# More buffers for adj's blocks and signs, a fifth group of kept products, and new costs in the planner of a two-layer graph kernel

## The chip, the cores and the metric

The kernel runs on one core of a Trainium2 chip. The metric is the device time of one execution in microseconds (us), the median of three runs. A core has a matrix engine (TensorE: PE for its matmuls, PEld for its weight loads in the profile), three engines for elementwise work (VectorE = DVE, ScalarE = ACT, GpSimd = POOL), a queue that issues transfers (SyncE = SP), and 16 DMA engines that carry the transfers of all queues.

## What is computed

Inputs are `x` (2708 nodes, 256 features, float32) and a sparse matrix `adj` (2708 by 2708) whose entries are zero or lie in 0.05 to 1, with a full diagonal. There are two layers. Cut to what matters:

```
# layer 0
A  = adj without its diagonal,  d = diagonal
n1 = GRU_edge(A @ x,  x)                          # gates from support @ Wih.T and x @ Whh.T
for each of 3 heads:  hW = x @ W;  hp = (A > 0) @ hW
    e = leaky_relu([hp, 0] @ a);  att = softmax(where(A > 0, e, very negative))
    s += (att * A) @ hW
n2 = GRU_node(s / 3, x)
x  = layernorm(x + d * n1 + d * n2)
# layer 1
h  = x @ W (4 heads of 64);  e = leaky_relu(src_i + dst_j) where adj_ij > 0.5
x  = layernorm(x + softmax_over_i(e).T @ h + bias)
```

A GRU cell needs six products for each of its 256 features: support times `Wih` and x times `Whh`, for each of three gates (r, z, n). The x products don't depend on the graph, so they can be made at any time once `x` and `Whh` are on the chip.

## The kernel before, in words

The 2708 nodes make 22 blocks of 128 (`NB`), and the blocks make six groups of up to 512 columns (`CH`; the last is 148 wide). The work has three stages, though they overlap.

**Stage 1, the sweep over adj.** For each group `g` and each pair of row blocks, 11 pairs to a group, a block of 2 x 128 x 512 of the transposed adj (512 KB) is loaded into `at2`. ScalarE makes two bf16 signs of it: `over2` (entry over a half) and `mask2` (entry nonzero). In between, GpSimd clears the diagonal in the blocks that have it. VectorE takes a maximum for each 64 columns (`found0`). TensorE multiplies `only` by `over2` into the bank `dbs[0]` and `u3` by `mask2` into `accs[0]`. After a group, `logits`, `flags` and `listed` turn the sums into lists of the rows that are nonzero in each 64-column tile (`idx0`), so that later stages gather these rows alone. Buffers: `at` has 4, `over` 2 and `mask` 2, all in the 24 KB-a-partition region `home1`.

Beside the sweep, `keep` makes x's GRU products of the first `KEPT` = 4 groups: for each of 2 cells, 2 halves of the features and 3 gates, two float32 matmuls of 128x512 into `accs[1]` or `dbs[1]`, in turn; a copy to one of three `kept` buffers (ScalarE for two of three, VectorE for the third); and a 256 KB store to `XH` in HBM. The weights `Whh` are loaded early; the weights `Wih` (`w_i`, 768 KB for each of the two cells) sit in the list `loads`, which the sweep empties one entry a pair, although they are first used by stage 2.

**Stage 2, layer 0.** For each 64-column tile, rows of x (with the attention weights) are gathered from HBM by index (POOL `rows`), scaled by the entries (`prepared`), and multiplied into `accs` (`multiplied`), the denominators into `dbs`; `divided` ends a tile. The first tile takes `accs[0]` and `dbs[0]`, the second `accs[1]` and `dbs[1]`, and so on in turn, so the second tile can't start before the last `keep` has left its banks. When the tiles of a group are done, `cells_and_norm` multiplies by the head weights (`supports`: 12 matmuls), runs both GRU cells, normalises, and writes the table for layer 1. A group below `KEPT` reads its x products back from `XH` and adds them on VectorE; a group from `KEPT` on makes them on TensorE.

**Stage 3, layer 1.** The same for 128-column tiles: gather, four weightings on VectorE for each tile of rows (`weighed`), four matmuls (`attended`), normalise, store.

**The order.** No engine's order is written out by hand. Every operation is first recorded by a `Plan`, with what it reads and writes (`note`), and a duration and a latency from `Plan.cost`. `Plan.issue` then plays a simulated clock: at each step it takes the engine that is free first and, among its ready operations, the one with the longest remaining chain, with a bonus for TensorE to stay with the operand type that it has (`STAY`) and a charge for changing it (`SWITCH`). That fixes the order of the instructions on each engine; on the chip an engine works through its list and waits when an operand isn't there. The constants matter for the change: `LOAD` (latency of a transfer), the latency of an indirect gather, and TensorE's costs by type and size. Since all instructions are emitted from the one call in the recorder, the profile gives every one of them the line L217 (or L1842 for the frame); they are told apart by tile names and shapes. `home1` to `home4` all appear as `f_home`.

Of the kernel before, what the change touches and what calls it, by code (L numbers as in the profile page):

```python
# [10 lines left out]
F32 = mybir.dt.float32  # L11
BF16 = mybir.dt.bfloat16
# [8 lines left out]
P = 128  # L21
D = 256
KD = D // P
HEADS0 = 3
HEADS1 = 4
C1 = D // HEADS1
# [4 lines left out]
CH = 512  # L31
# [67 lines left out]
class Plan:  # L99
# [7 lines left out]
    JOINED = 16  # L107
    ENGINES = ("tensor", "vector", "scalar", "gpsimd", "sync")
    LAG = 0.08
    LOAD, RATE, QUEUED = 2.2, 250.0e3, 4.0  # L110
    SWITCH, STAY = {"scalar": 1.3, "tensor": 0.2}, {"tensor": 5.0}
    TABLES = {AF.Sigmoid: 1, AF.Tanh: 1, AF.Exp: 2, AF.Sqrt: 3}

    def __init__(self, nc):
# [36 lines left out]
    def cost(self, engine, method, out, ins, kwargs):  # L151

        n = max(self.count(v) for v in [out] + ins)
        if method == "indirect_dma_start":
            return 1.25, 3.0
        if method == "dma_start":
            size = 4
            for _, k in tuple(out.ap):
                size *= k
            return 0.08 if engine == "sync" else 0.25, self.LOAD + size / self.RATE  # L160
        if engine == "tensor":
            n = self.count(out)
            if ins[0].dtype == BF16:
                t = max(0.06, n / 2000)
            else:
                t = max(0.22 if ins[0].ap[-1][1] <= C1 + 1 else 0.43, n / 590)
            return t, t + 0.1
        by_partition = any(isinstance(kwargs.get(k), bass.AP) for k in ("bias", "scale"))
        if engine == "scalar":
            t = 0.09 + n / 1200 + 0.1 * by_partition  # L170
        elif engine == "gpsimd":
            t = 0.1 + n / (1300 if method == "memset" else 320)
        elif method == "reciprocal":
            t = 0.07 + n / 160
        else:
            pairs = all(v.dtype == BF16 and tuple(v.ap)[-1] == (1, 2) for v in [out] + ins)
            t = 0.06 + n / (1900 if pairs else 3800 if method == "memset" else 960)
            t += 0.065 * (method == "scalar_tensor_tensor")
        return t, t + 0.08
# [127 lines left out]
def fast_path(ctx: ExitStack, tc: tile.TileContext, i: dict, out: bass.AP, bad: bass.AP):  # L307
# [11 lines left out]
    nc = plan = Plan(tc.nc)  # L319
# [27 lines left out]
    const = ctx.enter_context(tc.tile_pool(name="f_const", bufs=1))  # L347
# [3 lines left out]
    def ring(tiles):  # L351

        return cycle(tiles).__next__
# [14 lines left out]

    TS = dram.tile([NG, HEADS1, CH], F32, name="f_TS")

    KEPT = 4
    XH = dram.tile([KEPT * 2 * KD * 3 * P, CH], F32, name="f_XH")
    plan.pitch = {XH.tensor.name: CH, T0.tensor.name: TW, T1.tensor.name: TW, TS.tensor.name: HEADS1 * CH}

# [73 lines left out]
    for t, of in ((less_room, TILES0 + TILES1), (less_whole, WHOLE0 + WHOLE1)):  # L448
        c = 0
        while c < len(of):  # L450
# [4 lines left out]
            c = e  # L455
# [237 lines left out]
    ap, tiles = Rings(const, 1, home2), Rings(const, 8, home1)  # L693
# [47 lines left out]
    def later_kd(src, wide, name):  # L741
        t = const.tile([P, KD, wide], F32, name=name)
        later(t, src.rearrange("(k p) n -> p k n", p=P))
        return t

    cells = []
    of_cells = ("edge", "node")
    w_hs = [later_kd(i[f"L0_gnn_{cell}_WhhT"], 3 * D, f"f_{cell}_wh") for cell in of_cells]
    later(xn[:, :GR, :], x[: GR * P, :].rearrange("(b p) d -> p b d", p=P))
    for cell, w_h in zip(of_cells, w_hs):  # L750
        w_i = later_kd(i[f"L0_gnn_{cell}_WihT"], 3 * D, f"f_{cell}_wi")
        b_i = const.tile([P, 3 * KD], F32, name=f"f_{cell}_bi")
        b_h = const.tile([P, 3 * KD], F32, name=f"f_{cell}_bh")
        later(b_i, i[f"L0_gnn_{cell}_bihT"])
        later(b_h, i[f"L0_gnn_{cell}_bhhT"])
        b_s = const.tile([P, 3 * KD], F32, name=f"f_{cell}_bs")
        cells.append((w_i, w_h, b_i, b_h, b_s))
# [48 lines left out]
    def head_weights(b0, b1):  # L806
        e = e_col[:, b0:b1, :]
        v = small.tile([P, NB * HEADS0], F32, name="e_v")[:, : (b1 - b0) * HEADS0]
        v = v.rearrange("p (b h) -> p b h", h=HEADS0)
        nc.vector.scalar_tensor_tensor(e, e, SLOPE, e, op0=ALU.mult, op1=ALU.max)  # L810
        nc.vector.tensor_scalar(v, e, SHIFT0 + REACH0, SHIFT0 - REACH0, op0=ALU.min, op1=ALU.max)
        nc.scalar.activation(Ew[:, b0:b1, :HEADS0], v, AF.Exp, bias=shift)
        split3(
            small, [E3[:, b0:b1, s * HEADS0 : (s + 1) * HEADS0] for s in range(3)],
            Ew[:, b0:b1, :HEADS0], P, (b1 - b0) * HEADS0, f"E_rest{b1 - b0}",
        )
        full = min(b1, NF)
        if full > b0:
            nc.sync.dma_start(
                T0[b0 * P : full * P, D:].rearrange("(b p) e -> p b e", p=P), Ew[:, b0:full, :]  # L820
            )
        if b1 > NF:
            nc.sync.dma_start(T0[NF * P :, D:], Ew[: size[last], NF, :])
# [28 lines left out]
    def keep(g, n, o, gate):  # L852
# [10 lines left out]
    keeps = [  # L863
        (g, n, o, gate) for g in range(KEPT) for n in range(2) for o in range(KD) for gate in range(3)
    ]

    for g, cs in enumerate(groups):
        w = width[g]
        pe, pf = accs[0], dbs[0]
        c0, nf = base[g] // W0, w // W0  # L870
        for b0 in range(0, NB, 2):
            pair = [b0, b0 + 1]
            at2 = tiles.tile([P, 2, CH], F32, name="at", bufs=4)
            over2 = tiles.tile([P, 2, CH], BF16, name="over", bufs=2)
            mask2 = tiles.tile([P, 2, CH], BF16, name="mask", bufs=2)
            for b in pair:
                if g == 0 and b % GR == 0:
                    load_xT(b // GR)
                    projected_u(b // GR)
            if loads and (g > 0 or b0 in (10, 16)):  # L880
                loads.pop(0)()
            for _ in range(1 if g < 2 else 2):
                if g > 0 and keeps:
                    keep(*keeps.pop(0))
            whole = size[b0 + 1] == P
            if whole:
                rows_of = adjT[b0 * P : (b0 + 2) * P, base[g] : base[g] + w].rearrange("(s p) n -> p s n", p=P)
                nc.sync.dma_start(at2[:, :, :w], rows_of)
            else:
                for b in pair:  # L890
                    nc.sync.dma_start(
                        at2[: size[b], b - b0, :w], adjT[b * P : b * P + size[b], base[g] : base[g] + w]
                    )
            parts = [(P, slice(0, 2))] if whole else [(size[b], slice(b - b0, b - b0 + 1)) for b in pair]
            for p, s in parts:
                nc.scalar.activation(over2[:p, s, :w], at2[:p, s, :w], AF.Sign, bias=minus_half[:p])
            for b in pair:
                if b in cs:
                    p, o = size[b], b * P - base[g]
                    v = at2[:p, b - b0, o : o + p]  # L900
                    nc.gpsimd.tensor_mul(v, v, off_diag[:p, :p])
            for p, s in parts:
                nc.scalar.activation(mask2[:p, s, :w], at2[:p, s, :w], AF.Sign)
                b1, b2 = b0 + s.start, b0 + s.stop
                nc.vector.tensor_reduce(
                    found0[:p, c0 : c0 + nf, b1:b2].rearrange("p c b -> p b c"),
                    at2[:p, s, : nf * W0].rearrange("p b (c i) -> p b c i", i=W0), AX.X, ALU.max,
                    apply_absolute_value=True,
                )
                if nf * W0 < w:  # L910
                    nc.vector.tensor_reduce(
                        found0[:p, c0 + nf : c0 + nf + 1, b1:b2].rearrange("p c b -> p b c"),
                        at2[:p, s, nf * W0 : w].rearrange("p b (c i) -> p b c i", c=1), AX.X, ALU.max,
                        apply_absolute_value=True,
                    )
            for b in pair:
                p = size[b]
                nc.tensor.matmul(
                    pf[:NB, :w], lhsT=only[:p, b, :], rhs=over2[:p, b - b0, :w], start=(b == 0), stop=(b == last)
                )  # L920
            for b in pair:
                p = size[b]
                nc.tensor.matmul(
                    pe[:H3, :w], lhsT=u3[:p, b, :], rhs=mask2[:p, b - b0, :w], start=(b == 0), stop=(b == last)
                )
        logits(g, pe)
        flags(g, pf)
        if g == NG - 3:
            while loads:
                loads.pop(0)()  # L930
            weights()
        if g == NG - 2:
            head_weights(0, groups[-1][0])
        listed(0, *ranked[0][g])
    head_weights(groups[-1][0], NB)
    plan.urgent = 0.0
    for batch, made in ranked[1]:
        listed(1, batch, made)
# [24 lines left out]
    rows, ready = {}, {}  # L963
# [888 lines left out]
```

## Time and profile before

| what | value |
|---|---|
| time, median of 3 | 910.15 us (910.13 to 920.45) |
| span of the profiled execution | 912.4 us, mean granted TensorE clock 0.945 |
| PE busy | 792.7 us, 3911 instructions |
| PEld busy | 494.4 us |
| DVE busy | 613.6 us |
| ACT busy | 548.7 us |
| POOL busy | 526.6 us |
| DMA | 132.41 MB, mean 145 GB/s |

"Busy" is the time in which an engine has an instruction in it, and for TensorE neighbouring matmuls overlap, so its share overstates how full it is. A float32 matmul stands in the trace as two instructions, a bf16 matmul as one. The DMA share is the mean over the 16 DMA engines.

The stages can be placed by their landmarks: the last load of adj is issued at 209.6 us, the last store of a kept product at 250.0 us, the first matmul with the head weights starts at 325.3 us, and GpSimd's first gather for layer 1 after a long wait starts at 744.0 us.

### The profile page before, as it was taken

What the parts mean: (1) busy time and instruction counts of PE and PEld (TensorE: products, weight loads), DVE (VectorE), ACT (ScalarE), POOL (GpSimd) and SP (SyncE); (2) the same over time, 40 slices, a digit from 0 to 9 for tenths busy, and PEclk for the clock granted to TensorE, in tenths of its full rate; (3) what the DMA queues carried; (4) which work ended last, traced back from release to release, by engine and by line L of the source; (5) the groups of instructions that cost most, each with busy time, mean ns of one, the idle gap of its engine ahead of it and who ended that gap; (6) DMA issues with size and microseconds to landing.
All of it is one profiled execution on the core that took longest, in us unless ns stands there. A gap on an engine that the chain in (4) does not pass through costs nothing. (4 is left out here: it accounts for less than half of the span.)

```text
span 912.4 us, 14024 instructions
## 1 busy us (share of the span) xinstructions
PE 792.7 (87%) x3911; PEld 494.4 (54%) x3911; DVE 613.6 (67%) x2051; ACT 548.7 (60%) x1552; POOL 526.6 (58%) x613
## 2 busy tenths in 40 slices
PE   4987889798989899988988997999899879988783
PEld 3532333344566645665446544645644468877782
DVE  6676679785366558785486547639713658999993
ACT  3779788765477854675357734745742333166687
POOL 3047867776777777677777776761410023577640
PEclk9899999999999999797998998999999999999995
DMA  8888889776533434543374435322310024665541
GB/s 323 274 273 252 243 236 312 226 201 172 154 104 105 134 74 128 161 109 92 85 218 140 119 83 166 91 64 87 83 53 0 4 60 122 180 179 179 148 125 45
DMA packets 85047, 132.41 MB, mean 145 GB/s; under 512 B 21520, under 2 KB 43880, under 8 KB 84320
## 3 DMA queue, kind: packets, MB, share of 16 engines
q1 hardware_dynamic: 63712, 84.26, 29.2%
q0 software_dynamic: 20320, 45.59, 19.8%
q10 hardware_dynamic: 928, 1.57, 0.5%
q8 instruction: 33, 0.54, 0.2%
q14 instruction: 54, 0.44, 0.2%
HBM read 113.03 MB, written 21.12 MB: 147 GB/s over the span
## 5 line engine op out<-in xcount | busy, mean ns | idle before, releaser
L217 POOL DMA_INDIRECT rows<-f_T,f_idx x254 | 254.9, 1003 | 222.4 <-PE side L217 87.0
L217 PE MATMUL acc<-four,rows 128*128 128x256 f32 (+1 forms) x712 | 193.6, 412 | 10.1 <-DVE f_home L217 5.5
L217 ACT ACTIVATE four<-four,rows 128x64 f32<-128x64 f32 (+1 forms) x534 | 145.9, 337 | 44.4 <-DMA rows<-f_T,f_idx 19.5
L217 PEld LDWEIGHTS acc<-four,rows 128*128 128x128 f32 x712 | 136.4, 203 | 48.4 <-issue 12.8
L217 POOL DMA_INDIRECT raw<-in_adj_dram,f_idx x91 | 89.4, 982 | 27.6 <-issue 18.0
L217 DVE TENSOR_REDUCE f_found<-f_home 128x16 f32<-128x1024 f32 (+4 forms) x84 | 72.1, 883 | 11.3 <-POOL f_home L217 7.4
L217 POOL DMA_INDIRECT f_xn<-in_adjT_dram,f_idx x63 | 66.4, 1055 | 22.5 <-issue 17.4
L217 POOL DMA_INDIRECT f_home<-in_adjT_dram,f_idx x67 | 64.8, 967 | 24.1 <-issue 14.0
L217 ACT ACTIVATE f_home<-f_home,f_minus_half 128x1024 bf16<-128x1024 f32 (+3 forms) x72 | 69.5, 976 | 10.6 <-DMA f_home<-in_adjT_dram 5.0
L217 PE MATMUL acc<-f_home,rows 128*65 128x128 f32 (+2 forms) x512 | 66.4, 283 | 10.3 <-DVE f_home L217 7.3
L217 ACT ACTIVATE f_home<-f_home 128x1024 bf16<-128x1024 f32 (+3 forms) x72 | 62.6, 880 | 15.3 <-PE acc L217 9.6
L217 PEld LDWEIGHTS acc<-f_home,rows 128*65 128x65 f32 (+1 forms) x512 | 56.0, 141 | 17.3 <-DVE f_home L217 10.3
L217 PE MATMUL side<-f_home,f_node_wi 128*128 128x512 f32 (+1 forms) x144 | 61.2, 560 | 1.1 <-DVE f_home L217 1.0
L217 DVE SCALAR_TENSOR_TENSOR f_home<-pl,rows,f_m 128x128 f32<-128x128 f32 x196 | 55.1, 338 | 5.9 <-DMA rows<-f_T,f_idx 5.6
L217 PE MATMUL side<-f_home,f_gat_w 128*128 128x512 f32 (+1 forms) x144 | 55.9, 544 | 1.9 <-DVE f_home L217 1.9
L217 PE MATMUL side<-f_home,f_edge_wi 128*128 128x512 f32 (+1 forms) x144 | 57.5, 543 | 0.0
L217 DVE TENSOR_TENSOR f_home<-f_home,side 128x512 f32<-128x512 f32 (+1 forms) x56 | 36.6, 656 | 29.2 <-PE side L217 28.3
L217 PE MATMUL db<-f_home,rows 128*65 128x128 f32 x376 | 49.8, 284 | 5.6 <-DVE f_home L217 5.6
L217 PE MATMUL db<-f_home,f_only 128*22 128x512 bf16 (+2 forms) x132 | 40.5, 388 | 15.3 <-ACT f_home L217 14.1
L217 ACT ACTIVATE m<-four 128x64 bf16<-128x64 f32 (+1 forms) x181 | 40.3, 246 | 15.6 <-DVE four L217 14.3
L217 PEld LDWEIGHTS db<-f_home,rows 128*65 128x65 f32 x376 | 40.8, 140 | 10.9 <-DVE f_home L217 7.5
L217 DVE SCALAR_TENSOR_TENSOR f_home<-ls,rows,f_m 128x128 f32<-128x128 f32 (+1 forms) x168 | 45.9, 334 | 0.1
(223 smaller groups left out, 1433.1 us busy)
## 6 DMA issues: line engine op xcount, KB each, us to landing
f_home<-in_adjT_dram SPq DMA_DIRECT2D x50, 512.0 KB
f_XH<-kept SPq DMA_DIRECT2D x48, 256.0 KB
f_home<-f_XH SPq DMA_DIRECT2D x48, 256.0 KB
f_home<-f_TS SPq DMA_DIRECT2D x5, 1024.0 KB
rows<-f_T SPq DMA_DIRECT2D x33, 132.0 KB
rows<-f_T,f_idx POOLq DMA_INDIRECT x254
f_T<-f_home SPq DMA_DIRECT2D x21, 132.0 KB
f_T<-in_x_dram SPq DMA_DIRECT2D x3, 896.0 KB
```

The lines of the kernel that those rows point to most:

```text
L217: call = lambda: f(*args, **kwargs)
```

## The change

There are three parts.

1. *More in flight in the sweep.* `over` and `mask` get 3 buffers each instead of 2. `at` keeps 3 buffers of its own and gets two more in the memory of the two cells' `w_i`, so 5 instead of 4. `w_i` leaves the list of early loads and is loaded after the sweep, when that memory is free.
2. *Five groups kept.* `KEPT` goes from 4 to 5, so the x products of the group with index 4 (512 wide) are made in the sweep and read back, like those of groups 0 to 3.
3. *The planner's costs.* `LOAD` goes from 2.2 to 2.5 us, an indirect gather's latency from 3.0 to 4.5 us, a bf16 matmul from n/2000 (at least 0.06) to n/2400 (at least 0.035), a float32 matmul with wide weights from at least 0.43 to at least 0.26, a transpose to 0.11, and a change of type on TensorE from 0.2 to 0.13. These change no instruction, but the order of all of them.

```diff
-    LOAD, RATE, QUEUED = 2.2, 250.0e3, 4.0
-    SWITCH, STAY = {"scalar": 1.3, "tensor": 0.2}, {"tensor": 5.0}
+    LOAD, RATE, QUEUED = 2.5, 250.0e3, 4.0
+    SWITCH, STAY = {"scalar": 1.3, "tensor": 0.13}, {"tensor": 5.0}
...
         if method == "indirect_dma_start":
-            return 1.25, 3.0
+            return 1.25, 4.5
...
-            n = self.count(out)
+            n, rows = self.count(out), ins[0].ap[-1][1]
             if ins[0].dtype == BF16:
-                t = max(0.06, n / 2000)
+                t = max(0.035, n / 2400)
+            elif method == "transpose":
+                t = 0.11
             else:
-                t = max(0.22 if ins[0].ap[-1][1] <= C1 + 1 else 0.43, n / 590)
+                t = max(0.22 if rows <= C1 + 1 else 0.26, n / 595)
...
-    KEPT = 4
+    KEPT = 5
...
-        w_i = later_kd(i[f"L0_gnn_{cell}_WihT"], 3 * D, f"f_{cell}_wi")
+        w_i = const.tile([P, KD, 3 * D], F32, name=f"f_{cell}_wi")
...
+    next_at = ring(
+        [tiles.tile([P, 2, CH], F32, name=f"at{k}", bufs=1) for k in range(3)]
+        + [c[0].rearrange("p k n -> p (k n)")[:, : 2 * CH].rearrange("p (s n) -> p s n", s=2) for c in cells]
+    )
...
-            at2 = tiles.tile([P, 2, CH], F32, name="at", bufs=4)
-            over2 = tiles.tile([P, 2, CH], BF16, name="over", bufs=2)
-            mask2 = tiles.tile([P, 2, CH], BF16, name="mask", bufs=2)
+            at2 = next_at()
+            over2 = tiles.tile([P, 2, CH], BF16, name="over", bufs=3)
+            mask2 = tiles.tile([P, 2, CH], BF16, name="mask", bufs=3)
...
     head_weights(groups[-1][0], NB)
+    for cell, (w_i, *_) in zip(of_cells, cells):
+        nc.sync.dma_start(w_i, i[f"L0_gnn_{cell}_WihT"].rearrange("(k p) n -> p k n", p=P))
     plan.urgent = 0.0
```

## The prediction

> **What bounds the kernel now.** I read the busy times by stretch first, because the whole-span shares mix stages with different limits. Columns: stretch and its length, then PE, PEld, DVE, ACT and POOL busy with their counts, granted clock, DMA share and GB/s.
>
> ```profile
> 20.00:60.00 40.00, 38.19 (x179) 18.96 (x179) 30.47 (x100) 31.64 (x36) 3.92 (x7) 0.91 0.83 253
> 60.00:100.00 40.00, 31.26 (x188) 12.74 (x187) 22.13 (x39) 31.13 (x41) 29.57 (x30) 0.96 0.92 283
> 100.00:140.00 40.00, 34.76 (x146) 13.27 (x145) 31.98 (x63) 34.91 (x48) 28.52 (x32) 0.96 0.81 237
> 140.00:180.00 40.00, 34.47 (x149) 14.80 (x148) 33.47 (x66) 31.78 (x41) 30.75 (x32) 0.91 0.85 267
> 180.00:220.00 40.00, 34.86 (x163) 16.45 (x164) 28.38 (x79) 27.22 (x65) 30.09 (x34) 0.96 0.77 199
> 220.00:250.00 30.00, 27.75 (x90) 15.81 (x88) 10.56 (x36) 11.62 (x38) 19.68 (x23) 0.94 0.50 149
> 250.00:667.00 417.00, 376.68 (x1645) 239.44 (x1645) 270.15 (x902) 259.90 (x917) 288.19 (x290) 0.94 0.41 114
> 667.00:719.00 52.00, 52.00 (x124) 23.24 (x123) 13.06 (x25) 11.53 (x20) 1.12 (x2) 1.00 0.03 7
> 747.00:912.00 165.00, 132.71 (x1084) 115.82 (x1084) 144.15 (x639) 89.44 (x307) 84.84 (x89) 0.93 0.47 139
> ```
>
> The reader sees four regimes. In the sweep nothing is full: PE, ACT and DMA all stand near 80 to 90%. From 250 to 667 PE leads at 90%. From 667 to 719 PE works alone. Stage 3 is VectorE's (144 of 165 us) and the change doesn't touch its arithmetic.
>
> Second, the chain of waits: start, length, what.
>
> ```profile
> 597.78 24.23 PE side L217 x56
> ...
> 667.46 51.50 PE side L217 x120
> ```
>
> The last line is group 4's `cells_and_norm`: 120 instructions back to back, 0.429 us each, with nobody else on the path. It is the only stage in which the time is plainly the sum of one engine's instructions. The line before it shows group 3, whose x products were kept: the piece shown, 56 of its 72 instructions, took 24.23 us, again 0.43 us each.
>
> Third, the waits of the sweep (20 to 220 us), of the transfer queue and of ScalarE: who, for whom, total us, times, longest.
>
> ```profile
> SPq L217 <- DVE f_found L217: 75.7, 37, 6.4
> SPq L217 <- ACT f_home L217: 38.2, 35, 3.9
> ```
>
> ```profile
> ACT f_home L217 <- PE acc L217: 13.9, 8, 5.2
> ...
> ACT f_home L217 <- DMA f_home<-in_adjT_dram: 3.3, 5, 2.0
> ...
> ACT f_home L217 <- PE db L217: 2.2, 4, 1.3
> ```
>
> The loads wait 114 us for a block to be let go by its last readers, while ScalarE waits only 3.3 us for a block to arrive. ScalarE waits 16.1 us for TensorE to let go of a sign buffer. So the ring of signs costs more than the latency of loads.
>
> Fourth, where the kept products run now, from the timeline of PE near the end of the sweep:
>
> ```profile
> 229.13 1.03 PE L217 MATMUL acc<-four,rows 128*128 128x256 f32 x4
> 230.00 1.88 PE L217 MATMUL db<-f_xT,f_node_wh 128*128 128x512 f32 x4
> ```
>
> The keeps don't fit into the sweep even now: the last adj block is issued at 209.6 us, yet keeps go on to about 249 us, in turn with the first tile's sums. The second tile needs their banks. This is the crux: an added keep may simply push stage 2 later.
>
> **What the Trainium skill says.** "Perfetto Trace Analysis", Identifying the Most-Contended Engine, calls matmul busy time a poor measure because matmuls are pipelined; the trace agrees (four keep instructions show 1.88 to 1.98 us, but follow each other every 0.43 us), so PE has more room in the sweep than 85% suggests. The same page, Optimization Strategy, says that a repeating gap can mean too few buffers; the 16.1 us on sign buffers fit that. "TensorE: Matmul & The Clock Gate", Architectural detail, says ScalarE and VectorE take their queues strictly in order; so one sign waiting for a buffer also holds the copies of kept products behind it. "DMA: Bandwidth & Descriptors", Issuing engines are not separate DMA queues, says all queues share 16 DMA engines; the trace's 0.77 to 0.92 share in the sweep says more loads in flight can only fill what is left.
>
> **Part 1, five groups kept.** Late, it removes from group 4 the products of x: 4 units (2 cells, 2 halves), each 6 matmuls, 24 matmuls or 48 instructions. By the 51.50 / 120 of the chain that is 48 x 0.429 = 20.6 us, all on the path. It adds 8 additions on VectorE (0.683 us each in the row of 128x512 additions into `f_home`, 5.5 us), which lie beside PE: VectorE has 13.06 us in those 52. It adds 12 loads of 256 KB, where the DMA moves 7 GB/s. A unit then has 12 instructions, 5.15 us of PE, against 4.85 to 5.5 us of VectorE (three additions, one fused, three or four in the update, at 0.68 to 0.75); close, but group 3 kept PE's pace with the same shape. I take the late gain as 20 us, bounds 15 to 20.6.
>
> Early, it adds the same 48 instructions, 20.6 us of PE, with 8 ScalarE copies (0.575: 4.6 us), 4 VectorE copies (0.68: 2.7 us) and 3.1 MB of stores. In 20 to 220 us PE shows 200 - 173.5 = 26.5 us of idle time, and the overlap above hides more (0.25 us for each of the 48 keeps, 12 us). I assume that half of the visible idle, 13 us, can be used. So the early cost is 20.6 - 13 = 7.6 us; bounds: 20.6 (nothing is filled) and -5 (all 26.5 is).
>
> **Part 2, buffers.** A third sign buffer removes most of the 16.1 us of ScalarE's waits; a fifth block lets loads go up to one pair earlier. That isn't added again: it is what lets PE's idle time be used. Moving `w_i` takes 1.6 MB from the sweep against 3.1 MB of stores added: net 1.5 MB, 5.5 us at 267 GB/s if DMA bounded, which I put inside the 7.6. The late loads of `w_i` wait for the last readers of two blocks, near 212 us; behind them in SyncE's order are row loads of the first tiles and XH reads. At 6 us for both (1.6 MB at 267 GB/s), they have 100 us: the first product with `w_i` starts at 335.3. Cost nothing; hidden behind 61 gathered tiles of group 0.
>
> **Part 3, the planner.** The old plan overrated PE in the sweep. By its constants against the new: 220 sign matmuls (22 blocks, 5 wide groups, 2 signs) x 0.043 = 9.4 us, 66 small float32 ones (44 of `projected_u`, 22 of `logits`) x 0.17 = 11 us, some 460 list matmuls (22 for each of 21 lists) x 0.011 = 5 us, about 100 changes of type (my guess: some two a pair) x 0.07 = 7 us; 32 us less, more than the 20.7 that it sees added. So the new order will put keeps earlier, into time that existed all along. Gathers: the chain has
>
> ```profile
> 659.71 0.95 POOL rows L217
> ...
> 660.97 3.30 DMA rows<-f_T,f_idx
> ```
>
> that is about 1 us on GpSimd and 3.3 to land, 4.3 in all: 4.5 is right and 3.0 was not. ScalarE waited 15.4 us for gathered rows between 250 and 667, where PE has 417 - 376.7 = 40 us idle. With consumers placed where their data is, I take a fifth of it, 8 us; bounds -15 and +10, as an order is not a smooth thing.
>
> **Sum.** -20 + 7.6 - 8 = -20.4, so 910 - 20.4, about 889 us. Stage 3 as before.
>
> **Rivals.**
> *A, the keeps are only moved.* PE, not idle waiting, sets the sweep's end: for it, the dense 186 to 250 us and keeps that already overflow. Early +18, late -20, order -3: 905 us. Against it: the 26.5 us of visible and 12 us of hidden room on PE, together nearly twice the added 20.6.
> *B, everything frees.* The sweep was held by rings, all idle time fills: early -4, order -12, late -20: 874 us. For it the 114 us of SyncE's waits; against it DMA at 0.85.
> *C, slower.* The new order misplaces work: longer assumed gathers take row buffers (9 in all) earlier, the second tile starts 20 us late and 10 us of idle is added after it while the late stage gains only 20: 920 us. For it: keeps and bank turns are coupled; against: the constants move toward the trace.
>
> **Chances.** Forecast 0.45, B 0.30, A 0.17, C 0.08. Faster by over 2% means under 892: B, and the forecast but for 0.08 of it, 0.67. Within 2%: 0.08 + A = 0.25. Slower: C, 0.08. The range leaves out half of C and the edges: 872 to 906.
>
> **What would show it.** Right: 72 instructions of `side` in about 31 us for group 4 instead of 120; keeps with a higher density from 60 to 200 us and their last store near 255 us; SPq's wait for f_found well under 75 us; ScalarE's waits for PE acc and db under 5 us; first head-weight matmul at 325 to 335 us. Wrong: that matmul at 345 or later (A); or the 250 to 667 stretch with more than 45 us of PE idle (C); or a sweep that ends before 200 us (B).

## The result, and the profile after

The changed kernel takes 880.39 us (median of four, 874.74 to 885.27) against 914.39 us for the kernel before in the same comparison: a ratio of 0.962, 95% interval 0.953 to 0.972. It is 34 us faster, where 21 had been forecast. Ratios here are taken over the runs that lie within 1.5% of the fastest of their kernel, while a time in us is the median of all runs.

The six groups of layer 0 give a ruler that fits every kernel here: the start of the first matmul with the head weights (`f_gat_w`) of each group, read from the timeline of TensorE. The first column takes in the sweep and group 0's tiles; the differences after it belong to the following groups' tiles and cells. Profiled executions, us:

| stretch | before | after | change |
|---|---|---|---|
| start to head weights of group 0 | 325.3 | 331.7 | +6.4 |
| group 0 to group 3 | 272.4 | 247.0 | -25.4 |
| group 3 to group 4 | 69.6 | 69.4 | -0.2 |
| group 4 to group 5 | 73.4 | 56.3 | -17.1 |
| group 5 to the end | 171.7 | 171.4 | -0.3 |
| whole span | 912.4 | 875.8 | -36.6 |

So the sweep got longer, the fifth kept group shows at group 4, and the largest part is between groups 0 and 3. No instruction of these groups was added or removed; of the three parts of the change only the order should reach them.

The busy times by stretch, first in the changed kernel for stretches shown before, then that middle part in both kernels (stretch and length; PE, PEld, DVE, ACT, POOL busy; granted clock; DMA share; GB/s):

```profile
180.00:220.00 40.00, 34.03 (x189) 17.08 (x187) 25.90 (x81) 24.92 (x54) 29.84 (x31) 0.91 0.86 238
220.00:250.00 30.00, 27.64 (x121) 14.44 (x120) 22.50 (x72) 16.46 (x55) 21.24 (x22) 0.95 0.79 223
250.00:667.00 417.00, 390.80 (x1722) 248.11 (x1721) 272.88 (x905) 269.19 (x942) 317.00 (x314) 0.98 0.43 123
667.00:719.00 52.00, 45.77 (x207) 33.02 (x206) 37.35 (x124) 20.13 (x50) 20.86 (x22) 0.87 0.32 97
```

The kernel before, groups 0 to 3:

```profile
325.30:597.70 272.40, 246.54 (x973) 151.60 (x973) 177.48 (x588) 157.55 (x536) 200.39 (x204) 0.92 0.44 122
```

The changed kernel, the same groups:

```profile
331.70:578.70 247.00, 227.73 (x978) 143.86 (x978) 167.82 (x547) 154.55 (x525) 189.30 (x185) 0.97 0.43 125
```

Two columns matter, PE's busy time and the granted clock (the share of full speed that TensorE was given). PE's idle time fell from 25.9 to 19.3 us, 6.6 us. And the granted clock rose from 0.92 to 0.97: the share not granted is 0.08 x 272.4 = 21.8 us before and 0.03 x 247.0 = 7.4 us after, 14.4 us. Together 21.0 of the 25.4; the rest is taken up in the section on the clock below. The stretch that was expected to stand in 667 to 719 has moved: there PE is no longer alone.

The chain of waits of the changed kernel at group 4's cells:

```profile
648.11 24.30 PE side L219 x56
672.41 1.73 PE acc L219 x8
674.13 3.43 PE side L219 x8
```

The `x120` block of 51.50 us has become a block of 72 instructions, still at 0.43 us each, with tiles of the last group set between its parts.

The transfer queue's and ScalarE's waits from 20 to 220 us:

```profile
SPq L219 <- ACT kept L219: 38.8, 17, 3.6
SPq L219 <- DVE f_found L219: 36.9, 17, 10.2
SPq L219 <- ACT f_home L219: 27.7, 20, 4.6
SPq L219 <- DVE kept L219: 16.4, 7, 6.2
```

```profile
ACT f_home L219 <- PE acc L219: 9.8, 5, 5.0
...
ACT f_home L219 <- PE db L219: 5.9, 2, 4.1
```

The wait of loads for VectorE's last read has halved, but the queue now stands 55 us before stores of kept products whose copies aren't ready. ScalarE still waits 15.7 us for TensorE to let go of sign buffers, against 16.1.

### The profile page after: what moved, and what is told of

It is laid out like the page before. It is cut to its first block, busy times and chain, and to the rows that moved or that the text cites. A ratio compares the mean times of both kernels' runs of the same rounds, so it can differ in the third digit from the quotient of the medians.

```text
span 875.8 us, 14092 instructions
## 1 busy us (share of the span) xinstructions
PE 780.4 (89%) x3911; PEld 490.4 (56%) x3911; DVE 609.9 (70%) x2063; ACT 551.3 (63%) x1560; POOL 532.3 (61%) x613
## 5 line engine op out<-in xcount | busy, mean ns | idle before, releaser
L219 POOL DMA_INDIRECT rows<-f_T,f_idx x254 | 258.0, 1016 | 115.9 <-PE acc L219 26.8
L219 PE MATMUL acc<-four,rows 128*128 128x256 f32 (+1 forms) x712 | 187.9, 400 | 8.8 <-ACT four L219 5.7
L219 ACT ACTIVATE four<-four,rows 128x64 f32<-128x64 f32 (+1 forms) x534 | 143.3, 336 | 23.0 <-DMA rows<-f_T,f_idx 15.8
L219 PEld LDWEIGHTS acc<-four,rows 128*128 128x128 f32 x712 | 131.6, 196 | 45.8 <-ACT four L219 14.2
L219 POOL DMA_INDIRECT f_xn<-in_adjT_dram,f_idx x63 | 66.8, 1060 | 20.1 <-issue 16.6
L219 DVE TENSOR_TENSOR f_home<-f_home,side 128x512 f32<-128x512 f32 (+1 forms) x64 | 41.9, 658 | 32.4 <-PE side L219 31.2
L219 PE MATMUL side<-f_home,f_gat_w 128*128 128x512 f32 (+1 forms) x144 | 58.7, 569 | 2.0 <-DVE f_home L219 1.9
L219 ACT ACTIVATE m<-four 128x64 bf16<-128x64 f32 (+1 forms) x181 | 40.2, 246 | 28.1 <-DVE four L219 24.0
L219 POOL DMA_INDIRECT f_m<-in_adjT_dram,f_idx x33 | 31.9, 967 | 37.3 <-DVE f_rel L219 20.1
L219 PEld LDWEIGHTS db<-f_home,rows 128*65 128x65 f32 x376 | 39.0, 137 | 13.9 <-DVE f_home L219 5.9
L219 DVE TENSOR_REDUCE f_found<-f_home 128x16 f32<-128x1024 f32 (+8 forms) x52 | 43.7, 860 | 3.3 <-POOL f_home L219 3.3
L219 ACT ACTIVATE f_home<-f_home,f_minus_half 128x1024 bf16<-128x1024 f32 (+5 forms) x44 | 41.9, 965 | 5.8 <-PE db L219 4.1
L219 PEld LDWEIGHTS side<-f_home,f_gat_w 128*128 128x128 f32 x144 | 28.0, 208 | 30.1 <-issue 27.1
```

The costliest lines, as they stand in the source:

```text
L219: call = lambda: f(*args, **kwargs)
```

## The experiments

Theory at the start: three effects that add, an early cost, a late gain by the fifth group, and a gain by the order between the groups. Rivals: the granted clock as an accident of the run; or the buffers as the carrier of it all. The first six runs complete the eight combinations of the three parts.

**The fifth group alone.**

```diff
-    KEPT = 4
+    KEPT = 5
```

> KEPT = 5 alone, all else as before. My theory (two effects of the fifth group add up: 17 us saved in group 4's cells, paid for by keeps that push the first tiles back): without the new order and buffers the early cost is 12 to 20 us, the late gain 17 to 20, so 905 to 914 us and the first head-weight matmul at 337 to 345 us. Rival (the keeps fit in anyway and the whole saving is kept): 892 us, that matmul at 326 to 330.

Measured: 1.018 of the time before (1.010 to 1.026). The head weights of group 0 start at 346.7, 21.4 us later; group 4 to group 5 takes 54.6 instead of 73.4, 18.8 less; groups 0 to 4 lose 10 between them. It is slower than any case of the expectation. The late half is of the size I had; the early one is just over it, as if nothing of the keeps had fitted in; and the 10 us between the groups I didn't have at all.

**The new costs alone.**

```diff
-    LOAD, RATE, QUEUED = 2.2, 250.0e3, 4.0
-    SWITCH, STAY = {"scalar": 1.3, "tensor": 0.2}, {"tensor": 5.0}
+    LOAD, RATE, QUEUED = 2.5, 250.0e3, 4.0
+    SWITCH, STAY = {"scalar": 1.3, "tensor": 0.13}, {"tensor": 5.0}
...
-            return 1.25, 3.0
+            return 1.25, 4.5
...
+                t = max(0.035, n / 2400)
+            elif method == "transpose":
+                t = 0.11
             else:
+                t = max(0.22 if rows <= C1 + 1 else 0.26, n / 595)
```

> The planner's new costs alone, all else as before. My theory (the shorter time between the head-weight matmuls of group 0 and group 3, 247 us against 272 before, is the order's doing): 885 to 892 us, with that time at 245 to 252 us. Rival 1 (it is the granted clock, 0.98 against 0.94 in that stretch, which the order doesn't set): 908 to 914, with that time near 270 at a like clock. Rival 2 (it needs the buffers or the keeps): also above 905.

Measured: 888.18 us, 0.974 (0.966 to 0.982). Groups 0 to 3 take 244.3 us, 28.1 less, with no buffer and no kept group changed. The middle part comes with the order alone. But rival 1 was not simply wrong: this kernel, too, shows a higher clock there.

```profile
326.80:571.10 244.30, 225.94 (x969) 141.75 (x965) 166.27 (x551) 151.88 (x520) 182.49 (x177) 0.98 0.44 126
```

PE idles 18.4 us and lacks 0.02 of the clock, 4.9 us: 7.5 and 16.9 us less than before, 24.4 of the 28.1. Whether the clock moves with the order or is an accident of one profile is looked at below, over ten kernels.

**The buffers alone.**

```diff
-            at2 = tiles.tile([P, 2, CH], F32, name="at", bufs=4)
-            over2 = tiles.tile([P, 2, CH], BF16, name="over", bufs=2)
-            mask2 = tiles.tile([P, 2, CH], BF16, name="mask", bufs=2)
+            at2 = next_at()
+            over2 = tiles.tile([P, 2, CH], BF16, name="over", bufs=3)
+            mask2 = tiles.tile([P, 2, CH], BF16, name="mask", bufs=3)
```

> The buffers alone (5 blocks, 3 + 3 signs, Wih late), all else as before. My theory (they only make room for keeps in the sweep): first head-weight matmul 3 to 8 us earlier than 325 and 903 to 909 us. Rival (the loads' 114 us of waiting for buffers bounded the sweep): that matmul before 312 us and 895 us or less.

Measured: 1.004 (1.001 to 1.007). The last load of adj is issued at 198.0 instead of 209.6 us, so the loads did get ahead; but the head weights of group 0 start at 323.6, only 1.7 us earlier. With the old order, the sweep's loads don't set the start of stage 2. Both expectations missed: the time is 917.72 us, 9 above the upper end of mine.

**The fifth group and the buffers, old costs.** The two diffs above together.

> KEPT = 5 and the buffers, with the old costs in the planner. My theory: late gain 17 us, early cost 6 to 10, no gain between the groups: 900 to 906 us. Rival (the clock, or the buffers, carry the gain between the groups): 880 to 888 us as in the changed kernel.

Measured: 913.04 us, 0.999 (0.996 to 1.001): nothing, and 7 us above my range. The head weights of group 0 start at 326.9, so the buffers take back 19.8 of the fifth group's 21.4 us; the late 18.8 are there; but groups 0 to 3 take 278.8 (6.4 more) and 3 to 4 take 73.6 (4.0 more). The rival that let the buffers carry the middle gain falls for the old costs.

**The new costs and the buffers, four groups.**

> The new costs and the buffers, with KEPT = 4: the changed kernel without its fifth kept group. The new costs alone gave 0.974, everything 0.962. My theory (the fifth group gives about 10 us once the order finds room for its keeps): 885 to 892 us, group 4 alone again for about 51 us. Rival (the buffers give the rest): 876 to 882.

Measured: 875.83 us, 0.957 (0.949 to 0.965): the rival's side. Without its fifth kept group the changed kernel is not slower. Its chain has the old block back:

```profile
629.32 51.74 PE side L219 x120
```

but its head weights of group 0 start at 316.5, 15.2 us before those of the changed kernel. Group 4 to 5 takes 74.5 against 56.3, 18.2 more. So the fifth group gains 18.2 and costs 15.2 at the start; groups 0 to 3 also take 4.0 us more with it (247.0 against 243.0). What is left, 1.7 us of the profiled spans in its favour and 4.6 us of the medians against it, is under the spread of the times.

**The new costs and the fifth group, old buffers.**

> The new costs and KEPT = 5 with the old buffers. With the old costs the fifth group cost 1.018. My theory (the order places the keeps, the buffers do little): 878 to 885 us, the first head-weight matmul at 330 to 338. Rival (without the third sign buffer and the fifth block the keeps have no room, as with the old costs): 893 us or more, that matmul at 345 or later.

Measured: 877.79 us, 0.959 (0.949 to 0.970). My side of it: with the new order and the old buffers the fifth group delays the head weights of group 0 by 9.9 us (326.8 to 336.7), where it cost 21.4 with the old order. The eight combinations, ratio to the kernel before:

| | neither | fifth group | buffers | both |
|---|---|---|---|---|
| old costs | 1 | 1.018 | 1.004 | 0.999 |
| new costs | 0.974 | 0.959 | 0.957 | 0.962 |

The parts don't add. With the old costs the other two are worth nothing or less; with the new ones either brings about 1.5%, at the edge of the intervals of about 1% each way, and both no more than one.

**The gather's latency alone.**

```diff
-            return 1.25, 3.0
+            return 1.25, 4.5
```

> Only the gather's latency in the planner goes from 3.0 to 4.5, all else as before. My theory (scaling and matmuls that stood before their rows had landed are now placed later): most of the new costs' 0.974, so 890 to 900 us. Rival (the gain is in TensorE's costs): 908 to 914.

Measured: 0.986 (0.983 to 0.989), about half of the new costs' effect. The head weights of group 0 start 10.6 us earlier (314.7), groups 0 to 3 take 10.6 us less, and 6.5 us of it are lost again after that. The reason that I gave didn't hold: from 250 to 660 us ScalarE's wait for gathered rows is 23.7 us in this kernel and 15.0 before.

```profile
314.70:576.50 261.80, 235.23 (x976) 143.35 (x973) 172.69 (x570) 152.77 (x524) 201.27 (x197) 0.97 0.44 124
```

PE idles as long as before (26.6 against 25.9 us); the clock is 0.97 instead of 0.92, 13.9 us, which is more than the 10.6 gained there. Between groups 0 and 3, PE's wait for `rden_own` (a finished tile's reciprocals) went from 12.3 us, the longest 3.1, to 2.5, the longest 0.9. Other waits of PE grew in its place: for ScalarE's scaled entries (`four`) from 1.8 to 7.3 us, and one gather held it for 3.8. Before, and in this kernel (total us, times, longest):

```profile
PE db L217 <- DVE rden_own L217: 12.3, 10, 3.1
PE acc L217 <- ACT four L217: 1.8, 3, 0.9
```

```profile
PE acc L217 <- ACT four L217: 7.3, 8, 2.2
PE db L217 <- DMA rows<-f_T,f_idx: 3.8, 1, 3.8
PE db L217 <- DVE rden_own L217: 2.5, 6, 0.9
```

**TensorE's costs alone.** `SWITCH` and the block of matmul costs; `LOAD` and the gather stay.

> Only TensorE's costs and its change of type in the planner are new; the gather stays at 3.0 and LOAD at 2.2. My theory: a small part, 902 to 910 us, most of it before the first head-weight matmul. Rival (they are the gain): 888 to 893 us.

Measured: 905.28 us, 0.990 (0.981 to 0.998).

```profile
326.80:591.50 264.70, 243.58 (x977) 154.19 (x976) 171.47 (x561) 156.57 (x537) 190.86 (x185) 0.91 0.42 120
```

The other half: here groups 0 to 3 take 7.7 us less, and PE idles 21.1 us, 4.8 less, at about the old clock. None of it stands before the head weights of group 0 (326.8), where I had put it. The two products, 0.986 x 0.990 = 0.976, make the 0.974 of all new costs; `LOAD` is left with nothing that shows at this resolution.

**Is the clock the order's doing?** The clock record of the trace has two values, 1.0 and 0.5, in steps of 3.4 us. The timeline of PE in the kernel before shows one case:

```profile
393.31 1.99 PE L217 MATMUL acc<-four,rows 128*128 128x256 f32 x8
398.40 0.80 PE L217 MATMUL db<-rden_own,f_ones_f 64*128 64x192 f32 x2 [3.10 <-DVE rden_own L217]
399.13 3.43 PE L217 MATMUL acc<-four,rows 128*128 128x256 f32 x8
```

Eight matmul instructions take 1.99 us; PE waits 3.10 us for VectorE; the next eight of the same kind take 3.43 us. In slices of 3.4 us, PE's own busy time and the clock (sixth busy-or-clock figure after the length: 0.96, then 0.53):

```profile
395.50:398.90 3.40, 0.50 (x2) 0.29 (x2) 3.40 (x18) 0.00 (x0) 2.49 (x4) 0.96 0.17 40
398.90:402.30 3.40, 3.40 (x9) 2.48 (x8) 3.40 (x18) 2.89 (x7) 2.57 (x3) 0.53 0.44 119
```

I cut the full-speed stretches that begin between 60 and 800 us in ten profiles (before, after, and the eight runs above) into such windows, and noted PE's busy share in each and whether half speed came next:

| PE busy in the window | windows | followed by half speed |
|---|---|---|
| under 40% | 49 | 49 |
| 40 to 50% | 32 | 27 |
| 50 to 60% | 69 | 24 |
| 60 to 70% | 103 | 13 |
| 70 to 80% | 132 | 3 |
| 80% and more | 1723 | 0 |

"TensorE: Matmul & The Clock Gate", What's actually happening, in the Trainium skill describes this: the clock is halved after an idle window of about 3.4 us, and the window runs free. The trace agrees on half speed and 3.4 us, but the window needn't be idle: under 50% busy was enough in 76 of 81. The half-speed time between groups 0 and 3 was 31 to 44 us in the four kernels with old costs, 10 to 16 us in the four with all new ones, 17 us with the gather's alone and 48 us with TensorE's alone.

So the time between groups 0 and 3 has three parts: PE's idle time; what half speed costs, which is half of PE's busy time at half speed (the 21.8 and 7.4 us above count its idle time too); and the rest, which is PE's busy time as it would be at full speed. One profiled execution each, us:

| kernel | length | idle | lost to half speed | rest |
|---|---|---|---|---|
| before | 272.4 | 25.9 | 20.1 | 226.4 |
| gather's latency alone | 261.8 | 26.6 | 6.5 | 228.7 |
| TensorE's costs alone | 264.7 | 21.1 | 21.6 | 222.0 |
| all new costs | 244.3 | 18.4 | 4.7 | 221.2 |
| changed kernel | 247.0 | 19.3 | 6.5 | 221.2 |

In all ten profiles the lost part is 14.7 to 21.6 us where the gather's latency is the old one and 4.7 to 7.6 us where it is the new one. The rest is 226.4 to 229.0 us with TensorE's old costs and 219.8 to 222.0 us with the new ones. So the two halves of the new costs go with different parts: the gather's latency on half speed, TensorE's costs on the rest and on idle time. Some of the rest is only moved: in the changed kernel, 357 instead of 368 instructions of the tiles' row products fall into this stretch, about 3 us of them. With TensorE's costs alone it fell by 4.4 us with none of them gone; what shortened it wasn't traced.

The pattern is clear in this stretch only. Over the whole span, half speed takes 93 to 119 us in the four kernels with old costs and 75 to 93 us in the four with all new ones. Inside one kernel the mean clock tells little of the time: the correlation of the two is -0.5 over 39 runs of the kernel before, and -0.06 over 18 with the gather's latency alone.

That is a strong pattern, not a proof by intervention. All five orders with the new latency share the small loss, so it isn't the luck of one profile; but a kernel with filler work in its idle times, which would hold the clock up without another order, wasn't tried.

**The last four runs** were made on another chip, on which the kernel before took 1082.93 us. The changed kernel itself wasn't run there, so they can be compared with the kernel before and among themselves only. Single instructions of GpSimd and ScalarE last as long there (a row gather 1001 ns in the kernel with 4.4 against 1016 in the changed kernel, an entry scaling 336 in both). TensorE's are longer (429 ns against 400 for one of a row product), at a mean clock of 0.885 against 0.959; the link of busy windows and half speed is there too (69 of 69 windows under 40%, 4 of 428 from 80% on). And there are stalls whose releaser the profile can't name, of which the changed kernel's profile has none. In the kernel with 4.4:

```profile
ACT f_home L219 <- remote: 69.7, 9, 15.5
DVE f_home L219 <- remote: 27.6, 4, 21.8
DVE ids L219 <- remote: 14.5, 2, 11.3
```

What they are, and how much of the longer time is theirs, stays open.

*Another number for the same latency* (`return 1.25, 4.4`, in the changed kernel):

> The changed kernel with 4.4 instead of 4.5 for the gather's latency: a change with no meaning, to see how far the time moves when the order is merely another one. My theory: within 1% of the changed kernel, 872 to 889 us. Rival (single orders are luck): outside that, with the time between the head-weight matmuls of groups 0 and 3 over 255 us.

Measured: 0.981 (0.967 to 0.995), 1058.44 us. That is half of the gain that the changed kernel has on the first chip; whether the other half is lost to the chip or to the 4.4 can't be told. So the expectation can't be judged, and the rival, that a single order is luck, isn't tested by this run.

*A latency that is too long* (`return 1.25, 6.0`):

> The changed kernel with 6.0 instead of 4.5 for the gather's latency. Theory 1 (4.5 is right because rows land about 4.3 us after the gather starts; more is no better): 876 to 890 us. Theory 2 (any later placing of consumers helps in-order engines): 868 us or less, with ScalarE's waits for rows well under 10 us. Theory 3 (too long a latency starves the ring of nine row buffers): 892 or more.

Measured: 1.008 (1.003 to 1.014), 1085.99 us, 2 to 3% slower than with 4.4 on the same chip. That speaks for theories 1 and 3 and against "later is always better": ScalarE's waits for rows between 250 and 660 us are down to 1.4 us, as theory 2 had it, and no time is gained. (With 4.4 there are none at all on that chip.) It is one order against one other, so that the longer latency as such makes the order worse isn't shown, and theory 3's shortage of row buffers wasn't looked for.

*Six groups kept* (`KEPT = 6`):

> The changed kernel with KEPT = 6: the last group, 148 wide, is kept too. It moves 24 narrow matmuls, 48 instructions of about 0.125 us, 6 us, off the end of layer 0. My theory (moved one for one): 876 to 884 us. Rival (the last group's cells stand at the end of layer 0 where nothing else can run, so it is a plain gain): 870 to 874 us.

Measured: 1056.45 us, 0.981 (0.970 to 0.991), the same as five groups with 4.4 on that chip (0.981). The 6 us in question are less than the interval, about 1% each way, so the times don't decide between the two. In the profiles, group 5 to the end is 6.6 us shorter than with 4.4, and the head weights of group 0 start 14.5 us later, which is not a plain gain.

*Three groups kept* (`KEPT = 3`):

> The changed kernel with KEPT = 3. With the new costs and buffers, 4 groups gave 0.957 of the time before and 5 gave 0.962. My theory (a kept group moves about 17 us of TensorE from the late cells to the time before the first head-weight matmul, one for one, so the number kept hardly matters): 872 to 884 us, first head-weight matmul near 302, groups 3 and 4 about 51 us of cells each. Rival (keeps fill idle time, with an optimum at 4): 890 us or more.

Measured: 1074.09 us, 0.994 (0.991 to 0.998), 1.3% slower than five groups with 4.4 there. As a ratio that is the rival's side: the number kept has an effect at this end, and one for one is too simple. Four wasn't run there, so an optimum isn't shown.

## Why the prediction was right, and where its steps were not

The time lay in the range and on the forecast side; the sum was short by 16 us in the profile's terms, -20.4 against -36.6. That the range held is in part luck: the late gain was rightly argued, the early cost came out right by two errors that cancel, and the largest term was a third of its size. At 880 us the time lies nearer to rival B's 874 than to my 889, though B's shorter sweep didn't come. Term by term:

1. *Late gain, -20.* The mechanism was right and the instruction count exact: 72 in place of 120 at 0.43 us. Measured -17.1 in the changed kernel, -17.0 to -18.8 in the pairs of runs that differ in the fifth group alone. VectorE did keep up, as argued.
2. *Early cost, +7.6.* Measured +6.4: right as a sum, wrong inside. I let the keeps fill 13 us of PE's idle time and said that the buffers were only what made it usable. With new costs and buffers the fifth group costs 15.2 us, while the buffers without it are worth 10.3 (new costs, 326.8 to 316.5), and the new costs alone add 1.5. Against its late gain of 18.2 the fifth group by itself then brings next to nothing, and not the 12.4 of my terms. My rival A, "the keeps are only moved", was nearly true of this part, though not of the whole.
3. *Order, -8.* This is the failed term: -25.4 between groups 0 and 3. I took a fifth of PE's 40 us of idle time and put the clock at nothing, without a reason. PE's idle time did fall by 6.6, close to what I had. But windows of 3.4 us in which PE was under half busy were followed by half speed in 76 of 81 cases, and 13.6 us less was lost to that. The remaining 5.2 us are PE's busy time at full speed, about 3 of them work that moved to other stretches; this I had not at all. The lines that I showed before had the clock beside the idle time (0.94 in 250 to 667), and I read past them.
4. *Why the gather's latency helps.* I named ScalarE's waits for rows. With that cost alone they rose to 23.7 us while the kernel got faster. What fell was TensorE's waits of up to 3.1 us for a tile's reciprocals, and the half-speed stretches between groups 0 and 3, from seven to three. One of the seven follows such a wait (the lines at 393 to 399 us); that the others went for this reason is not shown, as other waits of PE grew and its idle time in all stayed.
5. *Sign buffers.* "Under 5 us" for ScalarE's waits on PE; measured 15.7. The third sign buffers help, but don't remove them: with the new costs and four groups they go from 33.6 to 23.2 us, with five from 26.4 to 15.7, and with the old costs and four from 16.1 to 13.1. The loads' wait for `f_found` did halve (75.7 to 36.9), but the queue's total stayed: kept copies took its place.
6. *The planner's room in the sweep.* "The new order will put keeps earlier" is wrong: of the keeps' instructions on TensorE, 136 of 192 start in the first 200 us before the change, 124 with the new costs alone, and 148 with the buffers alone. With five groups it is 162 of 240 with the old costs, 145 with the new ones, and 179 in the changed kernel. So the buffers bring keeps forward and the new costs put them back. The new order with five groups still ends group 0 10 us before the old one (336.7 against 346.7), for a reason that wasn't traced. The last store of a kept product is issued at 260.9, where I said near 255.
7. *Late load of `Wih`.* Nothing shows that it costs anything, as argued: issued at 218.8 us for the first cell and 236.8 for the second, first used at 342.0 and 359.7.

## What to carry to other kernels

Time in which the matrix engine waits may be paid twice, once as idle and once as slow clock after it. When a change breaks up or removes waits that leave the engine less than half busy over some 3.4 us, cost both, and read the clock column beside the busy column. Moving work from a full stage to an emptier one is a gain only by what the emptier one really absorbs: measure the move alone, as its late half is easy to see and its early half isn't. Where an order is planned from costs, it pays to correct them by the trace: in this kernel the new costs alone gave 2.6%, the buffers alone nothing, and the fifth group alone cost 1.8%. A latency set too long may hurt as well; one run on another chip points that way.

## What the runs showed of the hardware that I had not expected

Half speed on TensorE needs no idle window: a 3.4 us window that was 40 to 50% busy was followed by it in 27 of 32 cases. Another chip ran the kernel before in 1083 instead of 913 us. The kernels profiled there have a lower TensorE clock and stalls of up to 22 us that no recorded instruction ended, while single instructions of GpSimd and ScalarE last as long as on the first chip.
